# Attention weights of two heads in four turned by VectorE blocks and a DMA round trip

## The chip, the cores and the metric

One kernel runs on one core of one Trainium2 chip. The metric is the device time of a run in microseconds (us). A core has TensorE (PE in the profile; PEld is its loading of stationary operands), VectorE (DVE), ScalarE (ACT), GpSimd (POOL) and SyncE (SP), which issues nearly all of this kernel's DMAs. Everything is computed in 32-bit floats.

## The reference

The input x is 8 sequences of 256 tokens of 512 features; a second input is one row of 512 conditioning values per sequence. Four layers follow each other, each with a residual:

```
layer 0: h = rms-normed x, scaled by the condition
         q: 8 heads of 64, k and v: 1 head of 64 shared by all; rotary positions on q and k
         x += softmax(q k' / 8) v Wo
         x += (silu(h Wg) * (h Wu)) Wd                  inner width 2048
layer 1: h = layernorm(x), scaled and shifted by the condition
         q, k, v: 16 heads of 32;  q = q / |q| * exp(min(log scale, log 100)),  k = k / |k|
         x += gamma1 * (softmax(q k' + bias) v Wproj + b)
         x += gamma2 * (gelu(h Wfc1 + b) Wfc2 + b)      inner width 2048
layer 2: 16 query heads of 32, 4 key/value heads through a latent of 128, rotary, block mask
         x += softmax(masked q k') v Wo
layer 3: 8 experts of 64 features with an inner width of 256, layernorm, scale and shift, out projection
```

The bias of layer 1 is a 256x256 input. |q| and |k| are taken per head and token.

## The kernel before

All 8 sequences go through one stage after another: attention0, mlp0, attention1, mlp1, attention2, layer3. Activations x stay on the chip as 16 tiles of 128 tokens x 512 features. Tiles come from named pools, each with a number of slots (BUFS, L41): for instance "p" has 7 slots of 128x512, "ctxT" 6 of 128x256, "qk" 4, "wbig" 8 of 128x2048 for weights, and PSUM is split into "A" (4 banks, scores) and "C" (4 banks, all else). A tile that finds no free slot waits until the last reader of the oldest has finished. A scheduler orders the instructions of every engine from the order in which the program lists them and from the dependencies; within an engine they then run strictly in that order.

**The attention loop** (`attend`, L609) runs over sequences b and groups g of four heads: 2 groups a sequence in attention0, 4 in attention1 and attention2. For a group,

- `scored` (L645) multiplies queries by keys into four PSUM banks of 128 queries x (2 x 256 keys), one bank a head;
- `softmax` (L651) takes, per head and tile of 128 queries, the row's lowest value of minus the scores: one reduction on VectorE for attention0 (L659), a fused add-bias-and-minimum that also writes the negated scores to a "p" tile for the others (L667). ScalarE takes the exponential into "p" and sums the row (L672). The sums of the group are inverted (L678), turned (L682), and written to memory by a DMA (`spread`, L685), from which another DMA reads each row broadcast over a head's partitions (L690), into a free piece of a weight tile ("wqkv" in attention0, "wbig" later);
- `turned` (L697) turns one head's 128x512 weights on TensorE: four 128x128 transposes into a "C" bank (L702) and one copy back into the same "p" tile. The copy is on VectorE for even heads (L460) and on ScalarE for odd ones (L464);
- `weighted` (L709) multiplies the turned weights by the values (L717), and `divided` (L727) multiplies by the broadcast inverse into a "ctxT" tile (L732).

The loop is pipelined by hand. For each group it lists: scores of this group; the turning of the first two heads of the last group; the softmax of this group; a helping of other TensorE work; the turning of the last two heads of the last group; another helping; the weighted sum of the last group and its division; another helping. The helpings (`some`) draw on a queue of generators: the projections of the next sequence (`project0/1/2`), the output projection of the last one (`added` and the like), both with `product_steps` (L585). Each step of a generator tells its cost in us of TensorE; the helping is a fixed share of the sequence's total.

**The projection of attention1** (`project1`, L1334) handles two token tiles. For each it makes q, adds the bias, squares it on ScalarE (L1375) and sums per head on VectorE (L1376); then k, copied out of PSUM (L1373) and squared. The 16 sums of q and the 16 of k lie in one tile "ss" of 128x32. GpSimd takes the maximum with a small number, the power of minus one half (L1379) over all 32 columns, multiplies q's by its scale, and scales q and k (L1383). TensorE then turns q and k (L1355).

**The input of a stage** (`prepare`, L502) is normed x, features by tokens. For most sequences VectorE turns its 32x32 blocks in place (L515, 128x1024), four DMAs put it into memory (L520) and DMAs fetch it back so that the blocks stand where a full transpose would have them: one DMA of 512 KB for the MLPs (L533), eight of 64 KB for the attentions (L539). SP issues all of these in its own order, together with the spread DMAs and the loads of weights and x (L276).

**The MLPs** use a seven-product form of the 2x2 block product. Their right-hand operands are the pieces of hT and three sums of such pieces. The sums are kept in "ctxT" tiles, or in "qk" tiles for the first sequence (`blocked`, `blocked_again`). `mlp` (L892) makes the first products (L908), sums them in "p" tiles (`sums`, L922), and makes the second products (L955).

Of the kernel before, what the change touches and what calls it, by code (L numbers as in the profile page):

```python
# [32 lines left out]
P = 128  # L34
# [7 lines left out]
    "n": 4, "hT": 2, "qT": 2, "kT": 2, "v": 2, "ctxT": 6, "p": 7, "qk": 4, "row": 3, "wbig": 8,  # L42
# [46 lines left out]
PI_BELOW = 3.1415925  # L89

# [21 lines left out]
def layout(inputs):  # L112
# [10 lines left out]
    def grouped(w):  # L123
# [20 lines left out]
        "bias": np.ascontiguousarray(a["mask_1x1xSxS_ff0"].reshape(S, S)),  # L144
        "vec": np.ascontiguousarray(np.concatenate([vec[k] for k in VEC], 1)),
# [26 lines left out]
class Program:  # L172
# [50 lines left out]
    def setup(self):  # L223
# [40 lines left out]
        self.n_turn = 0  # L264
        self.half_pi = c([P, 1], "half_pi")
# [190 lines left out]
    def copy(self, i, out, in_, scale=None):  # L456

        if i % 2 == 0:
            if scale is None:
                self.nc.vector.tensor_copy(out, in_)  # L460
            else:
                self.nc.vector.tensor_scalar(out, in_, scale, None, ALU.mult)
        elif scale is None:
            self.nc.scalar.copy(out, in_)  # L464
        else:
            self.nc.scalar.activation(out, in_, AF.Copy, scale=scale)

    def modulated(self, i, out, in_, scale, shift):
        if shift is None:
            self.copy(i, out, in_, scale)  # L470
        elif i % 2 == 0:
            self.nc.vector.tensor_scalar(out, in_, scale, shift, ALU.mult, ALU.add)
        else:
            self.nc.scalar.activation(out, in_, AF.Identity, bias=shift, scale=scale)
# [27 lines left out]
    def prepare(self, name, b, quick=False):  # L502
# [14 lines left out]
        self.n_turn += 1  # L517
        to = kept.rearrange("(c i) (a x) -> a i c x", c=4, a=4)
        for a in range(4):
            nc.sync.dma_start(  # L520
                to[a], hT[32 * a : 32 * a + 32, :].rearrange("p (c x) -> p c x", c=4)
            )
        self.ready[name, b] = [hT, None, kept, 0]
# [17 lines left out]
    def h(self, name, b, quick=False):  # L541
# [16 lines left out]
        def placed(i, c, in_):  # L558
            scale = mod[:, scale_at + c, b : b + 1]
            shift = None if shift_at is None else mod[:, shift_at + c, b : b + 1]  # L560
            self.modulated(i, place[:, c], in_, scale, shift)

        if rows is None:
            for c in range(KC):
                placed(c, c, place[:, c])
# [43 lines left out]
    def attend(self, name, n_groups, hd, project, value, finish, work, key_tiles=(2, 2), biased=None,  # L609
# [27 lines left out]
        def scored(b, g):  # L637
# [3 lines left out]
            for j0 in range(0, 4, rows):  # L641
                for q in range(TB):
                    for j in range(j0, j0 + rows):
                        lhsT, rhs = lhs_rhs[j]
                        nc.tensor.matmul(  # L645
                            s[j][:, at[q] : at[q] + wide[q]], lhsT(q), rhs(wide[q]),
# [4 lines left out]
        def softmax(s):  # L651
            tot = self.t([P, 4, TB], "tot", 3)
            lows = self.t([P, 4, TB], "low", 3)
            ps = []
            for j in range(4):
                p = self.bank("p")[:, :total]
# [5 lines left out]
                for q in range(TB):  # L662
                    cols = slice(at[q], at[q] + wide[q])
                    src, sign = s[j], 1.0
                    if biased is not None:

                        nc.vector.tensor_tensor_reduce(  # L667
                            p[:, cols], s[j][:, cols], biased[:, cols], -1.0, BIG, ALU.add,
                            ALU.min, low[:, q : q + 1],
                        )  # L670
                        src, sign = p, -1.0
                    nc.scalar.activation(  # L672
                        p[:, cols], src[:, cols], AF.Exp, bias=low[:, q : q + 1], scale=sign,
                        accum_out=tot[:, j, q : q + 1],
                    )
                ps.append(p)
# [18 lines left out]
            return ps, by  # L695

        def turned(j, p):  # L697
# [9 lines left out]
            self.copy(j, p, m[:, :total])  # L707

        def weighted(b, g, pT):  # L709
            o = self.bank("C")  # L710
            for c in range(nch):
                for k in range(TB):
                    mine = [n for n, (kk, q) in enumerate(pairs) if kk == k]
                    q0 = pairs[mine[0]][1]
                    for i in range(per):
                        j = c * per + i
                        nc.tensor.matmul(  # L717
                            o[i * hd : (i + 1) * hd, c * S + q0 * P : (c + 1) * S],
                            value(got[b][1], g, j, k),
                            pT[j][:, mine[0] * P : (mine[-1] + 1) * P],  # L720
# [3 lines left out]
                        )  # L724
            return o
# [14 lines left out]
        for i in range(B * n_groups + 1):  # L740
# [17 lines left out]
            if last is not None:  # L758
                for j in range(2):
                    turned(j, last[2][0][j])  # L760
            if ahead is not None:
                ahead = (b, g, softmax(ahead[2]))
# [10 lines left out]
            elif ahead is None and then is not None:  # L773

                b, g, (pT, by) = last
                for j in range(2, 4):
                    turned(j, pT[j])
# [10 lines left out]
            else:  # L788
                self.some(quantum)
                b, g, (pT, by) = last  # L790
                for j in range(2, 4):
                    turned(j, pT[j])
# [58 lines left out]
    def blocked(self, b, hT):  # L851

        if b > 0:
            ts = [self.t([P, S], "ctxT") for _ in range(3)]
        else:

            ts = [t[:, i * S : (i + 1) * S] for t in (self.bank("qk"), self.bank("qk")) for i in range(2)]
            ts = ts[:3]
# [6 lines left out]
        return blocks  # L865

# [8 lines left out]
    def blocked_again(self, b):  # L875
# [3 lines left out]
        ts = [self.t([P, S], "ctxT") for _ in range(3)]  # L879
# [12 lines left out]
    def mlp(self, ups, downs, down_sums, load_ups, load_down, act, h, finish, tail):  # L892
# [29 lines left out]
        def sums(m):  # L922

            g = self.t([P, 4, P], "p")
# [4 lines left out]
            return g  # L929
# [69 lines left out]
        for s in range(n):  # L999
            hh, b, p = where(s)  # L1000
            w = ups[4 * hh + p]
            if p == 0:
# [4 lines left out]
                else:  # L1007
                    ms = [begun(i, x) for i in w]
                    gs = [sums(m) for m in ms]
# [10 lines left out]
            if s > 0:  # L1020
                ms = [begun(i, x) for i in w]
                gs = [sums(m) for m in ms]
# [213 lines left out]
    def layer0_mlp(self):  # L1236
# [52 lines left out]
        def finish(hh, b, ys):  # L1289
# [7 lines left out]
            (self.project1(0, self.got), 22.1),  # L1297
# [36 lines left out]
    def project1(self, b, got):  # L1334
# [28 lines left out]
        for t in range(TB):  # L1363
            ss = self.t([P, 32], "ss", 2)
            q = yield from part(t, 0)
            qs = self.bank("qk")
            nc.vector.tensor_tensor(qs, q, self.q_bias, ALU.add)
            sq = self.bank("n")
            nc.scalar.activation(sq, qs, AF.Square)
            nc.vector.tensor_reduce(ss[:, 0:16], heads(sq), AX.X, ALU.add)  # L1370
            k_ = yield from part(t, 1)
            ks = self.bank("qk")
            nc.scalar.copy(ks, k_)  # L1373
            sq = self.bank("n")
# [377 lines left out]
```

## Time and profile before

| what | value |
|---|---|
| median of 3 runs | 2128.06 us (2125.02 to 2128.92) |
| the profiled execution | 2125.73 us, its span 2123.8 us |
| granted TensorE clock, mean | 0.994 |
| moved by DMA | 138.18 MB |

| stage, us from the span's start | TensorE busy, us |
|---|---|
| start, 0 to 45 | 30.2 of 45 |
| attention0, 45 to 300 | 238.0 of 255 |
| mlp0, 300 to 890 | 590.0 of 590 |
| turn to layer 1, 890 to 920 | 28.8 of 30 |
| attention1, 920 to 1297 | 365.7 of 377 |
| mlp1, 1297 to 1667 | 370.0 of 370 |
| attention2, 1667 to 1975 | 293.2 of 308 |
| layer3, 1975 to 2124 | 144.6 of 149 |

A line of a group of instructions reads: line of the kernel, engine, operation, output<-input, partitions x elements, xcount | busy time in us, mean ns of one | idle time of the engine just before them, and what ended most of it. Matmuls overlap in TensorE's pipe, so the mean of one is longer than busy time over count. In a table of stretches each row has the stretch, its length, the busy time (and count) of PE, PEld, DVE, ACT and POOL, then TensorE's granted clock, the mean busy share of the 16 DMA engines and GB/s. A line of the timeline has the start, the duration of the piece, engine, line and what it is. A line of the waits has who waited for what, then us in total, times, the longest.

### The profile page before, as it was taken

The numbers are of one execution on the slowest core, as the hardware profiler recorded it, in microseconds if no ns is written. First come the engines' busy times: TensorE is split into PE (matmuls) and PEld (weight loads), VectorE is DVE, ScalarE is ACT, GpSimd is POOL, SyncE is SP. The second block draws the span as 40 slices with busy tenths as digits, with TensorE's granted clock in tenths as the row PEclk, the third lists the DMA queues.
The fourth block names the chain that finished last, engine by engine and source line by source line (L and its number), as shares of the span: only waits on it lengthen the run. The fifth ranks groups of instructions, "written<-read, shape, count | busy, mean of one in ns | idle before, by whom it ended". The sixth has DMA issues, their size and how long they took to land.

```text
span 2123.8 us, 36492 instructions
## 1 busy us (share of the span) xinstructions
PE 2060.5 (97%) x13282; PEld 1523.8 (72%) x13282; DVE 1349.5 (64%) x4474; ACT 761.1 (36%) x2330; POOL 291.3 (14%) x308
## 2 busy tenths in 40 slices
PE   7999899999999999999999999999999989999999
PEld 4555569999999999855555547999999855555444
DVE  6856665656676555756666665776666777776333
ACT  3424321111111111245555663222222256566644
POOL 1101100000000000144444432000000101010220
PEclk9999999999999999999999999999999999999999
DMA  8320241211230100411112132233211222210001
GB/s 308 115 59 17 91 149 38 73 41 58 76 94 19 36 19 18 100 46 40 37 40 52 44 95 78 85 102 115 94 49 46 76 47 45 57 39 19 11 35 40
DMA packets 172147, 138.18 MB, mean 65 GB/s; under 512 B 77824, under 2 KB 144064, under 8 KB 171968
## 3 DMA queue, kind: packets, MB, share of 16 engines
q1 hardware_dynamic: 171968, 135.86, 21.6%
q8 instruction: 105, 1.72, 0.3%
q14 instruction: 74, 0.61, 0.1%
HBM read 99.87 MB, written 35.95 MB: 64 GB/s over the span
## 4 chain that ended last, share of the span: by engine, by line
PE 81%; DVE 8%; DMA 5%; ACT 2%; POOL 2%; issue 1%; SPq 1%; DVEq 0%; ACTq 0%; POOLq 0%
PE C L908 28%; PE C L585 20%; PE A L955 18%; PE C L702 4%; PE A L645 4%; PE C L717 3%; DMA wqkv<-spread 2%; DVE p L667 1%; PE A L1621 1%; DMA spread<-invT 1%; ACT p L672 1%; PE C L1639 1%; DMA turn<-hT 1%; DMA hT<-turn 1%; DVE p L460 1%
## 5 line engine op out<-in xcount | busy, mean ns | idle before, releaser
L908 PE MATMUL C<-hT,wbig 128*128 128x128 f32 x3072 | 416.3, 275 | 0.0
L908 PEld LDWEIGHTS C<-hT,wbig 128*128 128x128 f32 x3072 | 388.8, 192 | 8.6 <-issue 1.8
L585 PE MATMUL C<-wqkv,hT 128*128 128x512 f32 (+1 forms) x768 | 311.1, 545 | 4.9 <-DVE p L460 3.9
L908 PE MATMUL C<-ctxT,wbig 128*128 128x128 f32 x2160 | 300.0, 275 | 0.0
L672 ACT ACTIVATE p<-p,low 128x256 f32<-128x256 f32 (+1 forms) x512 | 241.9, 475 | 152.7 <-DVE low L667 152.0
L908 PEld LDWEIGHTS C<-ctxT,wbig 128*128 128x128 f32 x2160 | 270.1, 192 | 0.0
L955 PE MATMUL A<-wbig,p 128*128 128x256 f32 x1024 | 242.5, 379 | 0.0
L585 PEld LDWEIGHTS C<-wqkv,hT 128*128 128x128 f32 x768 | 130.9, 191 | 124.7 <-issue 111.2
L667 DVE CUSTOM_DVE_ANT_0 p<-A,row 128x256 f32<-128x256 f32 (+1 forms) x512 | 171.7, 386 | 70.6 <-PE C L717 55.1
L955 PEld LDWEIGHTS A<-wbig,p 128*128 128x128 f32 x1024 | 189.6, 190 | 23.0
L702 PEld LDWEIGHTS C<-ident,p 128*128 128x128 f32 x1152 | 129.3, 142 | 81.3 <-issue 39.6
L925 ACT COPY p<-C 128x128 f32<-128x128 f32 x192 | 51.3, 267 | 371.6 <-PE C L908 370.9
L936 DVE TENSOR_TENSOR p<-p,C 128x256 f32<-128x256 f32 x192 | 79.3, 421 | 162.7 <-PE C L908 160.8
L702 PE MATMUL C<-ident,p 128*128 128x128 f32 x1152 | 165.2, 282 | 15.2 <-DVE p L460 6.8
L585 PE MATMUL C<-wo,ctxT 128*128 128x512 f32 x336 | 158.7, 604 | 5.6 <-DVE ctxT L732 5.5
L439 POOL TENSOR_SCALAR r<-mv 128x2 f32<-128x2 f32 (+1 forms) x28 | 7.2, 256 | 953.0 <-DVE mv L432 953.0
L1276 ACT ACTIVATE p<-C 128x128 f32<-128x128 f32 x64 | 17.8, 278 | 295.9 <-DVE p L936 295.9
L926 DVE TENSOR_TENSOR p<-p,C 128x128 f32<-128x128 f32 x192 | 54.9, 286 | 101.5 <-ACT p L925 99.4
L460 DVE COPY p<-C 128x512 f32<-128x512 f32 (+1 forms) x160 | 100.7, 630 | 23.8 <-PE C L702 23.4
L585 PEld LDWEIGHTS C<-wo,ctxT 128*128 128x128 f32 x336 | 58.7, 190 | 70.5 <-issue 53.8
L672 ACT ACTIVATE p<-A,low 128x256 f32<-128x256 f32 x128 | 59.3, 478 | 120.5 <-DVE low L659 87.9
L464 ACT COPY p<-C 128x512 f32<-128x512 f32 (+1 forms) x160 | 85.5, 535 | 36.0 <-PE C L702 36.0
(226 smaller groups left out, 3064.7 us busy)
## 6 DMA issues: line engine op xcount, KB each, us to landing
turn<-hT SPq DMA_DIRECT2D x120, 128.0 KB
hT<-turn SPq DMA_DIRECT2D x16, 512.0 KB
kept<-hT SPq DMA_DIRECT2D x16, 512.0 KB
hT<-kept SPq DMA_DIRECT2D x16, 512.0 KB
wbig<-spread SPq DMA_DIRECT2D x64, 128.0 KB
hT<-turn SPq DMA_DIRECT2D x112, 64.0 KB
wbig<-in_wada1T SPq DMA_DIRECT2D x6, 1024.0 KB
ctxT<-kept SPq DMA_DIRECT2D x48, 128.0 KB
```

Source lines behind the costliest of these rows:

```text
L460: self.nc.vector.tensor_copy(out, in_)
L464: self.nc.scalar.copy(out, in_)
L585: self.nc.tensor.matmul(out, lhsT(k), rhs(k), start=(k == 0), stop=(k == n - 1))
L645: nc.tensor.matmul(s[j][:, at[q] : at[q] + wide[q]], lhsT(q), rhs(wide[q]), start=True, stop=True,)
L667: nc.vector.tensor_tensor_reduce(p[:, cols], s[j][:, cols], biased[:, cols], -1.0, BIG, ALU.add, ALU.min, low[:, q : q + 1],)
L672: nc.scalar.activation(p[:, cols], src[:, cols], AF.Exp, bias=low[:, q : q + 1], scale=sign, accum_out=tot[:, j, q : q + 1],)
L702: nc.tensor.transpose(m[:, n * P : (n + 1) * P], p[:, at[q] + k * P : at[q] + (k + 1) * P], self.ident,)
L717: nc.tensor.matmul(o[i * hd : (i + 1) * hd, c * S + q0 * P : (c + 1) * S], value(got[b][1], g, j, k), pT[j][:, mine[0] * P : (mine[-1] + 1 ...
L908: nc.tensor.matmul(m[:, c : c + P], w[:, k * P : (k + 1) * P], b[:, k], start=(first and k == 0), stop=(k == steps - 1), skip_group_check= ...
L926: nc.vector.tensor_tensor(g[:, 0, :], g[:, 0, :], m[:, P : 2 * P], ALU.add)
L936: nc.vector.tensor_tensor(g[:, 1:3, :], g[:, 0, :].unsqueeze(1).to_broadcast([P, 2, P]), m[:, 2 * P : 4 * P].rearrange("p (i t) -> p i t", ...
L955: nc.tensor.matmul(acc[at][:, half * S : (half + 1) * S], left, right, start=(p == 0 and half == 0), stop=(p == 3), skip_group_check=True,)
```

## The change

In attention0 and attention1, for all sequences but the last, the first two heads of each group (`in_blocks`) are no longer turned by TensorE.

- `scored` multiplies these heads by keys in a permuted order (a strided view of the key tile).
- `softmax` writes their exponentials interleaved into one "p" tile of 128x1024, in four chunks of 64 columns for each query tile. VectorE turns its 32x32 blocks in place, four DMAs of 128 KB put it into memory (`put`, shared now with `prepare`), and one DMA of 512 KB reads it back into the same tile. These instructions are listed right after the softmax steps of the third head and before those of the fourth.
- `weighted` reads these heads' weights through a strided view of that tile (runs of 32), and these matmuls are kept in program order.
- `turned` is called once where it was called twice, and its remaining copies both go to ScalarE in those groups. Where no head is in blocks, the copies alternate as before.
- attention1's bias is needed in the permuted order too: a second copy (`bias_blocks`, prepared with the other inputs) is loaded into a piece of a weight tile of layer 1 that is free during the attention.

Around it: "p" has 4 slots of 128x1024 instead of 7 of 128x512; a group takes two, one for the heads in blocks and one for the others. The MLPs and layer3 take a pair of 128x512 tiles as one slot. "ctxT" goes from 6 slots to 4, and the MLPs' three operand sums take "ctxT" for odd sequences and "qk" for even ones (`three`). `layer1_begin` runs the first projection of attention1 and then loads one of layer 1's down weights and the bias; the other weights of layer 1 follow in the order ups, downs. In `h`, the in-place scalings of the input are kept in program order.

In `project1` the norms are apart: for q, and then for k, squares, sums, maximum, power over 16 columns and scaling follow each other at once. k's squares are taken from PSUM.

```diff
-    "n": 4, "hT": 2, "qT": 2, "kT": 2, "v": 2, "ctxT": 6, "p": 7, "qk": 4, "row": 3, "wbig": 8,
+    "n": 4, "hT": 2, "qT": 2, "kT": 2, "v": 2, "ctxT": 4, "p": 4, "qk": 4, "row": 3, "wbig": 8,
...
+    def in_blocks(self, name, b):
+        return 2 if name != "attention2" and b < B - 1 else 0
+
+    def put(self, kept, tile):
+        to = kept.rearrange("(c i) (a x) -> a i c x", c=4, a=4)
         for a in range(4):
-            nc.sync.dma_start(
-                to[a], hT[32 * a : 32 * a + 32, :].rearrange("p (c x) -> p c x", c=4)
+            self.nc.sync.dma_start(
+                to[a], tile[32 * a : 32 * a + 32, :].rearrange("p (c x) -> p c x", c=4)
             )
...
+                        keys = rhs(wide[q])
+                        if j < self.in_blocks(name, b):
+                            keys = keys.rearrange("p (k c i) -> p c k i", c=4, i=32)
                         nc.tensor.matmul(
-                            s[j][:, at[q] : at[q] + wide[q]], lhsT(q), rhs(wide[q]),
+                            s[j][:, at[q] : at[q] + wide[q]], lhsT(q), keys,
...
+            blocks = self.t([P, 8 * P], "p")[:, : 2 * total]
+            if n_blocks:
+                put = blocks.rearrange("p (c h x) -> p h c x", c=4, h=2)
+                ps = []
+            else:
+                ps = [blocks[:, j * total : (j + 1) * total] for j in range(2)]
+            plain = self.t([P, 2, 512], "p")
+            ps += [plain[:, j, :total] for j in range(2)]
...
-                ps.append(p)
+                if j == n_blocks == 2:
+                    nc.vector.transpose(blocks, blocks)
+                    kept = self.flips[self.n_flip % 4][:, : 2 * total]
+                    self.n_flip += 1
+                    self.put(kept, blocks)
+                    nc.sync.dma_start(blocks, kept)
...
+            came = blocks.rearrange("p (a h n j) -> p h n a j", a=4, h=2, j=32)
+            def weights(j, mine):
+                if j < self.in_blocks(name, b):
+                    ns = [at[pairs[n][1]] // P + pairs[n][0] for n in mine]
+                    step = ns[1] - ns[0] if len(ns) > 1 else 1
+                    return came[:, j, ns[0] : ns[-1] + 1 : step]
+                return plain[j - self.in_blocks(name, b)][:, mine[0] * P : (mine[-1] + 1) * P]
...
             if last is not None:
-                for j in range(2):
-                    turned(j, last[2][0][j])
+                weights = last[2][0][1]
+                for j, p in enumerate(weights[: len(weights) // 2]):
+                    turned(j + len(weights) % 4 // 2, p)
...
+    def three(self, b):
+        if b % 2 == 1:
+            return [self.t([P, S], "ctxT") for _ in range(3)]
+        two = [self.bank("qk") for _ in range(2)]
+        return [two[0][:, :S], two[0][:, S:], two[1][:, :S]]
...
+            both = []
+            for i in range(2):
+                m = yield from part(t, i)
+                y = self.bank("qk")
+                sq = self.bank("n")
+                if i == 0:
+                    nc.vector.tensor_tensor(y, m, self.q_bias, ALU.add)
+                    nc.scalar.activation(sq, y, AF.Square)
+                else:
+                    nc.scalar.activation(sq, m, AF.Square)
+                    nc.scalar.copy(y, m)
+                r = ss[:, 16 * i : 16 * i + 16]
+                nc.vector.tensor_reduce(r, heads(sq), AX.X, ALU.add)
+                nc.gpsimd.tensor_scalar(r, r, 1e-24, None, ALU.max)
+                nc.gpsimd.tensor_tensor(r, r, self.neg_half[:, 0:16], ALU.pow)
+                if i == 0:
+                    nc.gpsimd.tensor_tensor(r, r, self.sm, ALU.mult)
+                by = r.unsqueeze(2).to_broadcast([P, 16, 32])
                 nc.gpsimd.tensor_tensor(heads(y), heads(y), by, ALU.mult)
+                both.append(y)
...
+    def layer1_begin(self):
+        yield from self.project1(0, self.got)
+        self.ups, self.downs = [], []
+        self.layer1_down(0)
+        self.bias_blocks = self.downs[0][3]
+        self.nc.sync.dma_start(
+            self.bias_blocks.rearrange("p (q k) -> p q k", q=TB),
+            self.d["bias_blocks"].rearrange("(q p) k -> p q k", p=P),
+        )
```

## What the change does to the time: a prediction

> **What bounds the kernel now.** I read four views in this order: the page's shares and its chain that ended last, the busy table by stretches of time, the costliest groups, and the timeline of one group of heads.
>
> ```profile
> span 2123.8 us, 36492 instructions
> PE 2060.5 (97%) x13282; PEld 1523.8 (72%) x13282; DVE 1349.5 (64%) x4474; ACT 761.1 (36%) x2330; POOL 291.3 (14%) x308
> ...
> PE C L908 28%; PE C L585 20%; PE A L955 18%; PE C L702 4%; PE A L645 4%; PE C L717 3%; DMA wqkv<-spread 2%; DVE p L667 1%; PE A L1621 1%; DMA spread<-invT 1%; ACT p L672 1%; PE C L1639 1%; DMA turn<-hT 1%; DMA hT<-turn 1%; DVE p L460 1%
> ```
>
> TensorE works 97% of the span and its lines lead the chain; L702, the transposes of softmax weights, is itself 4% of it. Work taken off TensorE therefore shortens the end unless a wait takes its place.
>
> The shares are means over stages. In the two attentions that change (45 to 300 us and 920 to 1297 us) the table gives, per stretch, busy PE, PEld, DVE, ACT, POOL:
>
> ```profile
> 45.00:300.00 255.00, 238.04 (x1379) 142.17 (x1378) 171.10 (x483) 90.38 (x299) 36.88 (x63) 0.99 0.26 78
> ...
> 920.00:1297.00 377.00, 365.73 (x2138) 195.29 (x2135) 239.75 (x834) 213.13 (x663) 156.76 (x116) 0.99 0.20 52
> ```
>
> Here too PE leads: idle 17 us of 255 in the first and 11 of 377 in the second; DVE is at 67% and 64%, ACT at 35% and 57%, the DMA engines at 0.26 and 0.20. The second has 32 groups, so 11.8 us a group, of which DVE needs 7.5 and ACT 6.7. There is room for PE to get 1 us shorter per group before either becomes the bound.
>
> ```profile
> L702 PE MATMUL C<-ident,p 128*128 128x128 f32 x1152 | 165.2, 282 | 15.2 <-DVE p L460 6.8
> L515 DVE STREAM_TRANSPOSE hT<-hT 128x1024 f32<-128x1024 f32 x30 | 37.1, 1236 | 0.3
> L460 DVE COPY p<-C 128x512 f32<-128x512 f32 (+1 forms) x160 | 100.7, 630 | 23.8 <-PE C L702 23.4
> L464 ACT COPY p<-C 128x512 f32<-128x512 f32 (+1 forms) x160 | 85.5, 535 | 36.0 <-PE C L702 36.0
> ```
>
> **Part 1, the transposes removed.** Four heads a group need 16 transposes; two heads in blocks need 8 fewer. Attention0 has 2 groups and attention1 has 4 for each of seven sequences: 14 + 28 = 42 groups, 336 transposes. What one costs is read from the timeline (start, duration):
>
> ```profile
> 1100.45 1.15 PE L645 MATMUL A<-kT,qT 32*128 32x256 f32 x16
> 1101.52 1.09 PE L702 MATMUL C<-ident,p 128*128 128x128 f32 x8
> 1102.45 1.04 PE L1355 MATMUL C<-ident,qk 128*128 128x128 f32 x8
> ...
> 1120.45 1.07 PE L717 MATMUL C<-p,v 128*32 128x256 f32 x16
> ```
>
> Eight take from 1101.52 to the next start at 1102.45, 0.93 us or 116 ns each. The group's busy time over its count, 165.2/1152, is 143 ns. The 282 ns is the latency of one in the pipe. The Trainium skill ("TensorE: Matmul & The Clock Gate", Part 4: PE-mode transpose) gives about 275 ns for one in a kernel; that matches the latency column and would make the saving 336 x 0.275 = 92 us. The step between starts decides what a queue of them costs, so I take 0.117: **-39 us**, with 48 (at 143 ns) as the other end.
>
> The same skill speaks against the change: "VectorE: DVE Perf Modes", Rules for kernel authors, says to turn 128x128 on TensorE where PSUM will do, since VectorE turns only 32x32 blocks. In total work the row agrees: 8 transposes are 0.93 us of PE and two evacuations, while the new way is 1.24 us of DVE plus 1 MB of DMA. By the rule the change loses; by the shares above it trades the full engine's time for idle ones', so I follow the shares.
>
> **Part 2, VectorE and ScalarE.** Per group one DVE block transpose of 128x1024 is added (L515's own shape, 1.24 us). Of the four evacuations two go, and the remaining pair both goes to ACT: DVE loses two at 0.63 us = 1.26, ACT keeps its two. Net 0 for both. The chunked operands of L667, L672, the keys of L645 and the moving weights of L717 read runs of 32 elements. That such runs cost PE nothing shows in L908, which reads the input in runs (hT) and whole (ctxT):
>
> ```profile
> L908 PE MATMUL C<-hT,wbig 128*128 128x128 f32 x3072 | 416.3, 275 | 0.0
> ...
> L908 PE MATMUL C<-ctxT,wbig 128*128 128x128 f32 x2160 | 300.0, 275 | 0.0
> ```
>
> 416.3/3072 = 136 ns against 300.0/2160 = 139: nothing. For DVE and ACT no row compares the two; I take nothing, at most 10% of a group's four L667 and four L672 (4 x 0.35 + 4 x 0.50 = 3.4 us), 0.3 us, hidden under PE's 10.9.
>
> **Part 3, the trip through memory.** After the block transpose, SP issues four puts of 128 KB, then a read of 512 KB into the same tile; the weighted sum (L717) waits for it. The MLP inputs already make this trip in the same shapes; SP's rows there and the chain's row for such a read:
>
> ```profile
> 333.82 1.77 SPq L520 DMA_DIRECT2D turn<-hT  x4
> 337.55 0.34 SPq L533 DMA_DIRECT2D hT<-turn  x1
> ```
>
> ```profile
> 244.39 7.70 DMA turn<-hT
> 252.18 3.94 DMA hT<-turn
> ```
>
> From the first put to the read's issue 3.73 us, then 3.94 to landing. With 1.24 of DVE that is 8.9 us. In the timeline the exps of the first two heads end 3.6 us after the scores begin (1104.06), and DVE may first be at the third head's L667: some 4 to 4.5. A block is back 13 to 13.5 us after its group's scores begin. Before, the weighted sum starts 1120.45 - 1100.45 = 20.0 us after the scores. I summed the PE work that the changed order puts between the two, at the row durations: attention0 14.4, 36.5, then 15 to 28 us; attention1 14.6 for the first group, then 16.4 to 26.9, and 12.9 to 21.8 in the last sequence in blocks. So mostly the trip is hidden under PE's other work (L585 above all). If that cover is gone each group costs what is missing, up to the whole 8.9. Tight places:
> - attention0's first group (14.4): SP is still issuing loads of x until 40.1 us, ahead of the puts. I take +3 (0 to 6).
> - attention1's first group (14.6): +1 (0 to 3).
> - attention1's last block sequence (12.9 and 15.9): +3 together (0 to 5).
> The 7.70 row is a put that came slowly while other transfers ran. Such a trip, 13 us, would be late for most groups; one in seven is a guess worth 0 to 6, counted in the range alone.
>
> **Part 4, SP's queue.** Five more issues a group, about 0.45 each, 210 in all. A put waits for DVE, and the read for its puts; behind it stand the spread reads (L690) of the divisors and the fetches of the next input (L533/L539). In the middle of the second attention a set of eight fetches stands between the first put and the others, in the group with 26.9 us of cover: nothing. A spread read held back about 2 us hurts only where it is on the path already: the chain has wqkv<-spread at 2% of the span, reads of 7.9 to 8.1 us in attention0, and L732 waited 14.7 us for them in 5 places. Before PE runs dry the cover is ctxT's; I take +3 (0 to 8). The bytes: 42 MB more; 1 MB a group at the 338 GB/s of the first 45 us is 3.1 us per 10.9, raising the DMA share from 0.20 to under 0.5.
>
> **Part 5, buffers.** p becomes four pairs instead of seven singles, and a group's fourth head no longer takes the slot that the previous weighted sum frees:
>
> ```profile
> DVE p L667 <- PE C L717: 55.1, 44, 2.8
> ```
>
> That is DVE's wait. The chain gives DVE p L667 about 1.5% of the span (32 us), but this is its work as well as its wait, with PE still 97% busy; I take -2 (0 to -8). ctxT from six to four, with the MLP's operands alternating between ctxT and qk, and the pairs in the last layer: L908 has no idle before it; 0 (to +3).
>
> **Part 6, norms apart.** POOL's power on 128x32 takes 5.45 us (L1379), on the critical chain twice at attention1's start (897.90 and 906.00). Two of 128x16 halve the last: by L1379 at 32 columns and L440's 0.71 to 0.74 us at 2, 0.16 us a column, so 2.9 us. By then q's are done, and the scaled k is ready some 2.5 to 4 us sooner, with 2 x 1.05 of scaling (L1383) also split; elsewhere it is hidden: **-3** (0 to -4). The order of the layer1 loads and the 256 KB of permuted bias lie under the first MLP: 0.
>
> **Sum.** -39 -3 -2 +7 +3 = -34. The profiled execution took 2125.73 us (span 2123.8); 2125.7 - 34 = 2091.7. The median of the runs shown, 2128.06, is 2.3 above it: **2094**. Its own range: with 48 for the transposes, -5, and half of the delays, 2125.7 - 48 + 2.3 = 2080; with 39, -5, and every delay at its upper end (6 + 3 + 5 + 8 = 22), 2106.
>
> **Rivals.**
> - *The trip outlasts its cover (slower).* PE waits at the weighted sum in most groups because the puts and the read take as long as that 7.70 row plus 3.94, 13 us with the transpose, so blocks come back 18 us after the scores against a cover of 16 to 18. The gain of 44 over 42 groups is used up at a mean wait of 1.05 us; at 2 us it is 84 - 44 = +40, 2168. For: 512 KB out and in again per group, on the one queue that feeds everything. Against: the MLP trips of the same shape took 7.7 us in all.
> - *Gain lost to other engines.* PE becomes shorter, but in-order waits for ACT's copies (now both on one engine) and exps take most of it, since L702 already waited 15.2 us. At half a microsecond in each of 42 groups, 21: 2115. For: ACT's exps lag DVE by 0.5 us a head.
> - *More gain.* 143 ns a transpose and the freed p slot worth 8: -48 -8 -3 +5 = -54, 2074.
> That the change doesn't do what it says is excluded: the changed order lists eight fewer transposes in each of the 42 groups.
>
> **Numbers.** 0.2% (4 us) is about what a measurement of this kernel tells from no change. Likeliest 0.55; more gain 0.13; gain lost 0.13 (2106 to 2123); about equal 0.03; slower 0.16. Faster 0.81, same 0.03, slower 0.16. 2072 to 2130 leaves out the slower case and a part of the higher gain.
>
> **What would show it.** L702's count 816, its busy time near 117; the two stretches shorter by some 10 and 25 us; PE's idle time before L717 (3.0 + 1.0 us now) below 12 in all with the block's read as releaser. The prediction is wrong if that wait is over 40 us, if a spread read or fetch on SP's queue stops L732 or L585 in every sequence, or if L667 or L672 have become longer by over a tenth.

## The result: 2155.04 us, 1.3% slower

| kernel | median of the runs | profiled span | granted clock, mean |
|---|---|---|---|
| before | 2128.49 us (2125.02 to 2130.22) | 2123.8 us | 0.994 |
| changed | 2155.04 us (2152.83 to 2161.6) | 2154.1 us | 0.980 |

The ratio is 1.0132 (95% interval 1.0106 to 1.0158): 28 us slower, where 2094 us and a gain of 34 were forecast. The head of the changed kernel's page and its chain by line:

```profile
span 2154.1 us, 36247 instructions
PE 2074.1 (96%) x12946; PEld 1506.0 (70%) x12946; DVE 1347.1 (63%) x4432; ACT 750.3 (35%) x2330; POOL 303.4 (14%) x340
...
PE C L963 28%; PE C L599 21%; PE A L1012 18%; ACT p L705 6%; PE C L765 3%; PE A L663 3%; PE C L740 2%; PE A L1692 1%; POOL ss L1439 1%; DVE p L701 1%; PE C L1711 1%; DVE st L440 1%; ACT p L472 1%; PE C L315 1%; DVE n L618 0%
```

TensorE has 336 instructions less and is busy 14 us more. The exponentials on ScalarE (L705), 1% of the chain before (L672), are 6%. The groups that the prediction sized came out as it sized them:

```profile
L740 PE MATMUL C<-ident,p 128*128 128x128 f32 x816 | 122.2, 281 | 4.9 <-DVE p L469 2.0 <-ACT qT L473 1.5 <-ACT p L705 0.8
L710 DVE STREAM_TRANSPOSE p<-p 128x1024 f32<-128x1024 f32 x42 | 52.2, 1243 | 6.3 <-ACT p L705 5.8
L1439 POOL TENSOR_TENSOR ss<-ss,neg_half 128x16 f32<-128x16 f32 x32 | 93.6, 2926 | 2.7
```

816 transposes with 43 us less of busy time, a block transpose of 1.24 us, a power of 2.93. So the loss is elsewhere. By stretches (the columns are those of the first tables: PE, PEld, DVE, ACT, POOL, then clock and DMA):

```profile
0.00:284.30 284.30, 251.51 (x1370) 145.49 (x1370) 197.85 (x566) 105.23 (x344) 43.76 (x84) 0.96 0.53 168
910.50:1291.30 380.80, 364.38 (x1878) 176.74 (x1877) 239.81 (x806) 209.22 (x662) 164.32 (x142) 0.96 0.46 124
1704.50:2002.40 297.90, 275.65 (x1818) 155.27 (x1817) 196.65 (x883) 161.48 (x616) 32.45 (x40) 0.95 0.16 37
```

The stretches run from the start to the first MLP's first product, from attention1's first scores to the second MLP, and over attention2 to its last weighted sum. Before, the same three took 291.4, 368.6 and 273.3 us. The first gained 7. Attention1, with two thirds of the removed transposes, lost 12; attention2, where no head is in blocks, lost 24.6. And the clock fell: a mean of 0.980 over 2154 us is some 86 us at one half, against 26 before.

Where one sequence of attention1 begins, TensorE's and then ScalarE's timeline show the hole:

```profile
1158.34 1.15 PE L663 MATMUL A<-kT,qT 32*128 32x256 f32 x16
1159.42 1.98 PE L599 MATMUL C<-wqkv,hT 128*128 128x512 f32 x4
1161.33 1.78 PE L663 MATMUL A<-kT,qT 32*128 32x256 f32 x8
1164.40 1.22 PE L663 MATMUL A<-kT,qT 32*128 32x256 f32 x4 [1.29 <-DVE low L701]
1165.55 7.95 PE L599 MATMUL C<-wqkv,hT 128*128 128x512 f32 x12
```

```profile
1160.67 0.51 ACT L705 ACTIVATE p<-p,low 128x256 f32<-128x256 f32 x1 [1.54 <-DVE low L701]
...
1164.38 0.51 ACT L705 ACTIVATE p<-p,low 128x256 f32<-128x256 f32 x1 [0.16 <-DVE low L701]
1164.89 1.08 ACT L480 ACTIVATE hT<-hT,mod 128x256 f32<-128x256 f32 x2
```

The projection of the next sequence (L599 at 1165.55) needs that sequence's scaled input, half of which ScalarE makes (L480). ScalarE does so only after the eight exponentials of the group. Until then, but for the four products on VectorE's half (L599 at 1159.42), TensorE has no other work than the scores of the second group, drawn up behind those of the first; these wait for VectorE to empty the four score banks. The clock in and after that stretch:

```profile
1160.40:1163.80 3.40, 2.71 (x11) 1.06 (x9) 3.32 (x15) 3.13 (x13) 0.00 (x0) 1.00 0.36 127
1163.80:1167.20 3.40, 2.80 (x6) 1.34 (x7) 0.96 (x5) 2.00 (x6) 0.00 (x0) 0.51 0.61 153
1167.20:1170.60 3.40, 3.40 (x5) 1.35 (x4) 0.00 (x0) 0.00 (x0) 0.00 (x0) 0.50 0.64 196
```

It is half for the next two of these pieces, though TensorE is full in the second of them. In the kernel before, ScalarE scaled the same input at 1123.66 and 1126.35, a good 30 us before the scores at 1159.11.

One line of the diff ties the scaling there: `keep_in_program_order` on `placed`, in `h`, called the edge from here on. The scaling is listed after the softmax of the first group, and with the edge it can't move ahead.

### The profile page after: what moved, and what is told of

Same layout as the page of the kernel before. It is cut to its first block, busy times and chain, and to the rows that moved or that the text cites. A ratio compares the mean times of both kernels' runs of the same rounds, so it can differ in the third digit from the quotient of the medians.

```text
span 2154.1 us, 36247 instructions
## 1 busy us (share of the span) xinstructions
PE 2074.1 (96%) x12946; PEld 1506.0 (70%) x12946; DVE 1347.1 (63%) x4432; ACT 750.3 (35%) x2330; POOL 303.4 (14%) x340
## 4 chain that ended last, share of the span: by engine, by line
PE 79%; ACT 7%; DVE 7%; POOL 3%; DMA 2%; issue 1%; SPq 0%; ACTq 0%; DVEq 0%; POOLq 0%
PE C L963 28%; PE C L599 21%; PE A L1012 18%; ACT p L705 6%; PE C L765 3%; PE A L663 3%; PE C L740 2%; PE A L1692 1%; POOL ss L1439 1%; DVE p L701 1%; PE C L1711 1%; DVE st L440 1%; ACT p L472 1%; PE C L315 1%; DVE n L618 0%
## 5 line engine op out<-in xcount | busy, mean ns | idle before, releaser
L599 PE MATMUL C<-wqkv,hT 128*128 128x512 f32 (+1 forms) x768 | 327.6, 568 | 2.6 <-ACT hT L480 1.4
L705 ACT ACTIVATE p<-p,low 128x256 f32<-128x256 f32 (+1 forms) x512 | 240.4, 471 | 160.4 <-DVE low L701 153.4
L599 PEld LDWEIGHTS C<-wqkv,hT 128*128 128x128 f32 x768 | 136.2, 200 | 133.3 <-issue 116.8
L599 PE MATMUL C<-wo,ctxT 128*128 128x512 f32 x336 | 157.7, 603 | 2.7 <-DVE ctxT L782 2.7
L963 PE MATMUL C<-qk,wbig 128*128 128x128 f32 x1152 | 160.0, 275 | 0.0
L963 PE MATMUL C<-ctxT,wbig 128*128 128x128 f32 x1152 | 160.0, 275 | 0.0
L701 DVE CUSTOM_DVE_ANT_0 p<-A,row 128x256 f32<-128x256 f32 (+1 forms) x400 | 128.9, 376 | 43.6 <-PE C L765 29.4
L963 PEld LDWEIGHTS C<-qk,wbig 128*128 128x128 f32 x1152 | 144.1, 192 | 0.0
L963 PEld LDWEIGHTS C<-ctxT,wbig 128*128 128x128 f32 x1152 | 144.1, 192 | 0.0
L740 PEld LDWEIGHTS C<-ident,p 128*128 128x128 f32 x816 | 93.0, 142 | 64.9 <-issue 40.8
L740 PE MATMUL C<-ident,p 128*128 128x128 f32 x816 | 122.2, 281 | 4.9 <-DVE p L469 2.0
L663 PE MATMUL A<-kT,qT 32*128 32x256 f32 (+2 forms) x896 | 105.6, 404 | 16.2 <-DVE low L701 12.5
L663 PEld LDWEIGHTS A<-kT,qT 32*128 32x128 f32 (+1 forms) x896 | 62.4, 191 | 67.0 <-issue 37.2
```

Source lines behind the costliest of these rows:

```text
L599: self.nc.tensor.matmul(out, lhsT(k), rhs(k), start=(k == 0), stop=(k == n - 1))
L663: nc.tensor.matmul(s[j][:, at[q] : at[q] + wide[q]], lhsT(q), keys, start=True, stop=True,)
L701: nc.vector.tensor_tensor_reduce(out, src, by, -1.0, BIG, ALU.add, ALU.min, low[:, q : q + 1])
L705: nc.scalar.activation(out, src, AF.Exp, bias=low[:, q : q + 1], scale=sign, accum_out=tot[:, j, q : q + 1],)
L740: nc.tensor.transpose(m[:, n * P : (n + 1) * P], p[:, at[q] + k * P : at[q] + (k + 1) * P], self.ident,)
L963: nc.tensor.matmul(m[:, c : c + P], w[:, k * P : (k + 1) * P], b[:, k], start=(first and k == 0), stop=(k == steps - 1), skip_group_check= ...
```

## The experiments

Theory A: the edge costs the time. Theory B: the blocks cost it (their trip through memory, their tiles). Every kernel here computes the whole reference. Ratios are to the kernel before on the same chip; 0.1% is 2.1 us.

### The edge added to the old kernel, and taken from the new one

old_pin, the kernel before with these lines and the change's `three`:

```diff
-    ... "ctxT": 6, "p": 7, ...
+    ... "ctxT": 4, "p": 8, ...
-                placed(c, c, place[:, c])
+                self.tc.keep_in_program_order(placed(c, c, place[:, c]))
```

> The kernel before with one new thing: the in-place scaling of a stage's input is kept in program order (to be schedulable at all it gets one more p slot, 8 instead of 7, and ctxT 4 with the changed kernel's sharing of operand sums). No head is in blocks and the norms are together. Theory A (the program-order edge on the scaling makes the scheduler pull the second group's scores of each sequence up behind the first's; TensorE then waits for VectorE to empty the score banks, and its clock drops): attention2 longer by about 21 us as in the changed kernel, attention1 longer by 15 to 25, half-clock time some 45 us more; 2160 to 2172 us. Theory B (the loss comes with the blocks: their DMA trip, their pair tiles): 2124 to 2132.

2183.06 us, 1.0259 (1.0238 to 1.028). Theory A, and more than it asked for: attention1 took 396.9 us, attention2 296.5. But half-clock time rose by 28 us only (mean clock 0.987 over 2177.4), where 45 were expected. What the slots have of the loss comes below.

new_unpinned, the changed kernel with:

```diff
-                self.tc.keep_in_program_order(placed(c, c, place[:, c]))
+                placed(c, c, place[:, c])
```

> The changed kernel with that one program-order edge taken away, all else as changed. Theory A: attention2 back to about 268 us and attention1 down from 381 to about 345 to 355; 2105 to 2120 us. Theory B: 2150 to 2160, attention1 still near 381 us.

2112.8 us, 0.9939 (0.9915 to 0.9963). One line is worth 1.9%, 41 us; without it the change is a gain. Attention1 falls from 380.8 to 348.5 us, attention2 from 297.9 to 281.5:

```profile
913.90:1262.40 348.50, 342.30 (x1880) 169.05 (x1879) 243.50 (x806) 207.55 (x662) 164.03 (x142) 0.99 0.51 138
1675.60:1957.10 281.50, 260.42 (x1818) 144.53 (x1817) 196.19 (x883) 159.31 (x616) 32.36 (x40) 0.98 0.17 40
```

new_noblocks, the changed kernel with `in_blocks` returning 0:

> The changed kernel with no head in blocks anywhere: TensorE turns all four heads, no trip through memory; slots, program-order edges and norms as changed. Theory A: attention2 stays near 290 us, attention1 near 390; 2155 to 2172 us. Theory B: about the time before, 2120 to 2132.

2186.77 us, 1.0276 (1.0252 to 1.0299). Slower than with blocks, by 31 us: theory B falls. It was above theory A's range too.

### Is it the scores drawn up, or the late scaling?

new_ordered, the changed kernel with:

```diff
-                        nc.tensor.matmul(
+                        self.tc.keep_in_program_order(nc.tensor.matmul(
                             s[j][:, at[q] : at[q] + wide[q]], lhsT(q), keys,
                             start=True, stop=True,
-                        )
+                        ))
...
-        nc.scalar.activation(sin[0], ang, AF.Sin, scale=-1.0)
+        self.tc.keep_in_program_order(nc.scalar.activation(sin[0], ang, AF.Sin, scale=-1.0))
```

(the latter for all four activations of `angles`)

> The changed kernel with the matmuls of the scores kept in program order too, and the four sine and absolute-value activations of the angle tables kept in program order on ScalarE (in the changed kernel they stand ahead of the copy of v and ScalarE waits 16.4 us there, TensorE 10.3). Blocks stay. Theory A: no pulled scores, half-clock time back to about 30 us, no 10 us hole near 60 us; the 39 us of transposes then show: 2090 to 2105 us. Theory B: only the hole at the start goes; 2138 to 2148 us.

2176.34 us, 1.0228 (1.021 to 1.0246): a miss, slower than the changed kernel. With the scores held back, TensorE simply stands until the scaling is done. Its wait for it before the projections, changed kernel first, then new_ordered:

```profile
PE C L599 <- ACT hT L480: 3.4, 6, 1.6
```

```profile
PE C L599 <- ACT hT L480: 29.0, 7, 4.3
```

Nor did half-clock time fall: it is 92 us (mean clock 0.979 over 2173.6). So scores drawn up are what the scheduler fills the hole with, and a little help; the late scaling makes the hole. The theory had the right line of the diff and the wrong link.

scaled_early keeps the edge and lists the scaling earlier:

```diff
             if ahead is not None:
+                if g == 0 and ahead_of and 0 < b < B - 1:
+                    next(self.queue[0])
                 ahead = (b, g, softmax(ahead[2], b))
```

> The changed kernel, its program-order edge on the input's scaling kept, but in attention1 and attention2 the scaling is listed before the softmax of a sequence's first group instead of after it. Theory A2 (the edge costs because the scaling must stand behind that group's eight exps on ScalarE, so the next sequence's projection comes late and TensorE has nothing else): the loss goes though the edge stays, 2105 to 2120 us, no half-clock stretch per sequence. Theory A1 (any such edge ties the engines' order too tightly): 2145 to 2160 us.

2106.74 us, 0.99 (0.9883 to 0.9916): 48 us less than the changed kernel, with the edge in place. Its timeline at the same point of the work:

```profile
1136.17 1.09 ACT L480 ACTIVATE hT<-hT,mod 128x256 f32<-128x256 f32 x2
1136.36 0.27 PE L740 MATMUL C<-ident,p 128*128 128x128 f32 x1
1136.57 1.15 PE L663 MATMUL A<-kT,qT 32*128 32x256 f32 x16
1137.64 2.84 PE L599 MATMUL C<-wqkv,hT 128*128 128x512 f32 x6
...
1138.20 0.51 ACT L705 ACTIVATE p<-p,low 128x256 f32<-128x256 f32 x1 [0.93 <-DVE low L701]
```

Scaling, scores, projection, and the exponentials meanwhile. The half-clock time is 44 us in place of 86.

### What the blocks, the norms and the slots are worth

unpinned_noblocks is new_unpinned with `in_blocks` returning 0.

> The changed kernel without the edge and with no head in blocks: what is left are the slots, the load order and the norms apart. If the prediction's term for the transposes is right (336 at 0.117 us less a few us of waits, 30 to 40 us between this and the same with blocks at 2112.8): 2140 to 2153 us. If the trip and the waits eat half of it: 2125 to 2135 us. If these other parts cost nothing it is at the time before, 2128.

2155.74 us, 1.0129 (1.0112 to 1.0147), against 0.9939 with blocks: 1.9%, 40 us, where the prediction's term for the transposes was 39. But with neither blocks nor edge the rest of the change costs 27 us, though its norms gain. So the 40 are what the blocks are worth beside that rest, not the transposes alone.

unpinned_norms_together is new_unpinned with `project1` as before.

> The changed kernel without the edge, and with the norms of queries and keys together as before. If the norms apart are worth the 3 us of the prediction at attention1's start: 2114 to 2118 us. If POOL's latency was hidden: 2110 to 2114 us.

2120.82 us, 0.9962 (0.9947 to 0.9977) against 0.9939 (0.9915 to 0.9963): about 5 us for the norms apart, with intervals that overlap. The expectation counted from the 2112.8 of another chip's runs; the ratios are what compares.

old_slots is the kernel before with 8 p slots, ctxT 4 and `three`; old_ctxT4 the same with 7 p slots:

```diff
-    ... "ctxT": 6, "p": 7, ...
+    ... "ctxT": 4, "p": 8, ...      (old_slots)
+    ... "ctxT": 4, "p": 7, ...      (old_ctxT4)
```

> The kernel before with 8 single p slots instead of 7, ctxT 4 instead of 6 and the shared operand sums of the MLPs; nothing else. unpinned_noblocks took 27 us more than the kernel before though its norms are worth 8 us less. If the freer slots are what costs it (groups run ahead, and the copies and divisions meet in VectorE's queue): 2145 to 2165 us. If it is the pair tiles or the load order of layer 1: 2126 to 2131 us.

> The kernel before with ctxT 4 instead of 6 slots and the shared operand sums of the MLPs, p left at 7. If the eighth p slot cost the 25.7 us of old_slots (TensorE's order here is that of the kernel before): 2124 to 2131 us, within 0.2% of before. If ctxT did: 2145 to 2152 us.

old_slots: 2150.77 us, 1.0114 (1.0099 to 1.0129). old_ctxT4: 2130.15 us, 1.0004 (0.9995 to 1.0013). So one more p slot, 2 KB a partition more to work in, costs the kernel before some 23 us. The edge alone, old_pin against old_slots, costs it 31. Who waits for whom, kernel before first, then old_slots:

```profile
PEld C L717 <- ACT p L464: 4.3, 9, 0.8
DVE ctxT L732 <- PE C L717: 6.2, 6, 1.6
```

```profile
PEld C L717 <- ACT p L464: 28.0, 38, 1.3
DVE ctxT L732 <- PE C L717: 35.1, 34, 3.8
```

With the slot free, the fourth head's exponentials no longer wait for the last group's weighted sum; they run ahead of the last group's copies in ScalarE's order, and the weighted sum (L717) waits for those copies. The matmuls of the weighted sums show it, kernel before first, then old_slots, then new_unpinned:

```profile
L717 PE MATMUL C<-p,v 128*32 128x256 f32 (+2 forms) x896 | 69.3, 370 | 3.0 <-DVE p L460 3.0
L717 PE MATMUL C<-p,kT 128*32 128x128 f32 (+2 forms) x384 | 34.2, 351 | 1.0 <-DVE p L460 1.0
```

```profile
L717 PE MATMUL C<-p,v 128*32 128x256 f32 (+2 forms) x896 | 81.6, 375 | 8.0 <-DVE x L1197 3.5 <-ACT p L464 2.9 <-DVE p L460 0.3
L717 PE MATMUL C<-p,kT 128*64 128x256 f32 (+2 forms) x384 | 36.9, 359 | 3.2 <-ACT p L464 2.4 <-DVE p L460 0.5
```

```profile
L765 PE MATMUL C<-p,v 128*32 128x256 f32 (+2 forms) x896 | 81.1, 372 | 7.7 <-ACT p L472 4.6 <-DMA p<-flip 1.7 <-DVE p L469 0.3
L765 PE MATMUL C<-p,kT 128*64 128x256 f32 (+2 forms) x384 | 36.7, 356 | 4.0 <-ACT p L472 3.9
```

Busy and idle time together are 107.5, 129.7 and 129.5 us. The same matmuls cost 22 us more in both; in unpinned_noblocks, where the slots are free too, they come to 127.2.

slots_back is early_first_plain (next part) with p's slots as tight as before:

```diff
-    ... "ctxT": 4, "p": 4, ...
+    ... "ctxT": 6, "p": 3, "pb": 2, ...
-            blocks = self.t([P, 8 * P], "p")[:, : 2 * total]
+            blocks = self.t([P, 8 * P], "pb")[:, : 2 * total]
-            plain = self.t([P, 2, 512], "p")
...
+                if j >= 2:
+                    ps.append(self.bank("p")[:, :total])
```

(the MLPs and layer3 take pairs and singles in turn)

> early_first_plain (0.9889 of before) with p's slots as tight as before: two pairs for the heads in blocks and three singles for the others, so that a group's fourth head again waits for the weighted sum before it; ctxT 6. If freer slots cost the changed kernel too (exps of the next group stand ahead of the copies and the division of the last): 5 to 20 us less than early_first_plain, the weighted sums back to 63 and 49 ns a matmul; 2082 to 2096 us. If only the kernel before, with more copies, pays for them: 2098 to 2104 us.

2108.88 us, 0.9909 (0.9894 to 0.9925) against 0.9889 (0.9868 to 0.9911): no gain. Attention1 and attention2 took 2.6 and 4.6 us less in the profile, but the stretch to the first MLP took 7 us more and that from the first MLP to attention1's scores another 7. The weighted sums did become cheap again: 105.2 us busy, against 118.7 in early_first_plain. But TensorE now waits for what comes from memory, for the block's reads and for divisions that wait for their spread reads:

```profile
PE C L599 <- DVE ctxT L782: 11.9, 6, 4.3
...
PE C L765 <- DMA pb<-flip: 7.1, 5, 3.0
```

In early_first_plain these were 2.0 and 0.3 us. So with blocks in, tight slots save at one place and lose as much at others: the slots that let the groups run ahead seem to be also what covers the trip. That rests on this one arrangement of the slots, with ctxT back at 6 besides.

slots_back_copy moves the second copy of a group with blocks to VectorE; slots_back_unpinned drops the edge and lists the scaling late again.

> slots_back with the second copy of a group with blocks on VectorE. If the copies' wait on ScalarE came from the freer slots: within 3 us of slots_back. If it is ScalarE's own load: 3 to 6 us less than slots_back.

> slots_back without the edge on the scaling and with the scaling listed where the changed kernel has it. If the edge costs only through its place: within 4 us of slots_back. If ScalarE and VectorE wait in order for a scaling whose DMA is late (26.9 us in 16 places in new_unpinned): 4 to 10 us more than slots_back.

2103.44 us, 0.9888 (0.987 to 0.9905); and 2117.6 us, 0.9953 (0.9938 to 0.9968). The copy's 0.2% lies within the intervals. The edge, with the scaling listed early, is worth 9 us against no edge: here a fixed place ahead of the exponentials is better than the place that the scheduler chose. And slots_back_unpinned, which has neither edge nor freed slots, is only 10 us faster than the kernel before, of which the norms have some 5. By that estimate, from three ratios, the blocks are worth about 5 us with tight slots, against the 40 with free ones.

### The first sequence and the copies

In the changed kernel TensorE stands 10.3 us near 57 us. unpinned_sine is new_unpinned with the activations of `angles` kept in program order.

> The changed kernel without the edge on the scaling, and with the four activations of the angle tables kept in program order on ScalarE. If ScalarE's 16 us wait for them is what makes TensorE stand 10.3 us near 57 us: that hole and half of its 10 us at half clock go, 2098 to 2104 us. If TensorE would wait there for the weights' trip anyway: 2109 to 2114 us.

2113.84 us, 0.9931 (0.9916 to 0.9946): no change. The copy of v came at once, and TensorE stood 8.43 us one step later, for VectorE's division (L782). In the changed kernel that division, of the first group, reads:

```profile
54.51 1.95 PE L765 MATMUL C<-p,kT 128*64 128x256 f32 x16
...
65.21 0.36 DVE L1153 TENSOR_SCALAR row<-row 128x384 f32<-128x384 f32 x1
65.48 0.75 DVE L782 TENSOR_TENSOR ctxT<-C,wqkv 128x256 f32<-128x256 f32 x2
```

Its weighted sum starts at 54.51 and its spread reads were issued at 47.77; the reads that SP issues late, at 58.69, are the second group's. VectorE works without a break from 53.73 up to the division: it stands behind the angle tables (L1133 to L1153) in VectorE's order. Why the scheduler puts it there is not shown. early_first_plain is scaled_early with the first sequence of attention0 turned by TensorE; early_first_copy adds the second copy on VectorE:

```diff
-        return 2 if name != "attention2" and b < B - 1 else 0
+        return 2 if name != "attention2" and b < B - 1 and (name, b) != ("attention0", 0) else 0
...
                 for j, p in enumerate(weights[len(weights) // 2 :]):
-                    turned(j + len(weights) % 4 // 2, p)
+                    turned(j, p)                         (early_first_copy)
```

> The kernel with the scaling listed early (2106.7 us against 2129.4 before), and with the very first sequence of attention0 turned by TensorE alone, as the last one is. If the first groups' trip, behind the loads of x on SP's queue, is what holds back the spread reads (issued at 59 us) and with them VectorE's division and TensorE for 10.3 us, plus the half clock after it: the hole near 57 us and 5 to 10 us of half clock go, 2092 to 2099 us. If the hole is due to the angle tables on VectorE and ScalarE alone: 2105 to 2110 us.

> As early_first_plain, and in groups with blocks the second of the two copies of turned weights goes to VectorE, the first stays on ScalarE. The weighted sums of attention1 take 77 ns a matmul in the middle and 108 in the upper quarter where 63 is undisturbed, some 9 us in the stage. If they wait for ScalarE's second copy, behind its exps: 5 to 9 us less than early_first_plain. If they wait for the block's read from memory: the same within 2 us, and the 108 ns stay.

2101.47 us, 0.9889 (0.9868 to 0.9911), and 2097.02 us, 0.9865 (0.9847 to 0.9882), on one chip with 2125.03 before. The hole is gone, and the first group's division comes at 59.19, but the stretch to the first MLP is only 3.4 us shorter in the profile (281.0 against 284.4); by the ratios the run can't be told from scaled_early. The copy's 4.4 us lie within the intervals too; but the weighted matmuls of attention1 are busy 40.5 us where they took 44.8 (37.6 before), so part of their wait was ScalarE's copy and not the read. early_first_copy beats both kernels, by 1.35% the one before.

## Why the prediction was wrong

**The step that failed first is not in the sum.** The edge on the input's scaling was told of with the change and priced nowhere: part 2 asked what VectorE and ScalarE have to do, not what stands ahead of what on them. It costs 41 us with blocks (1.0132 against 0.9939) and 31 without (1.0276 against 1.0129), enough to turn -34 into a loss.

**It is not the whole miss.** Without the edge the change gains 13 us of the 34. The 21 that are missing are of the size of the 22 us more at the weighted sums, which part 5 had with the wrong sign; that the two are the same is read from the traces, not tested. A rival, "gain lost to other engines", foresaw this part: it said 2115 us by in-order waits for ScalarE's copies and exponentials, and new_unpinned took 2112.8. None of the rivals was the edge.

**Part 1 was right on the transposes themselves.** L740's busy time is 43 us less, against 39. That 40 us lie between unpinned_noblocks and new_unpinned is in part luck, since the worth of the blocks depends on the slots. In both pairs that differ in the blocks alone, with the edge (31 us) and without, the blocks gain: the rule to turn on TensorE does not hold here, where TensorE is full.

**Part 2.** The rates were right. L701 in chunks, whose bias lies in wbig, takes 419 ns, and 418 whole; L705 takes 497 on average (501 before), and in attention0, where almost half of it is in chunks, 485 (478 before). So chunks of 64 in runs of 32 cost next to nothing. "Net 0" for the copies was not right: both copies on ScalarE wait behind its exponentials. early_first_copy puts that at some 4 us, within the noise.

**Part 3 was right for the changed kernel, and the slower rival wrong.** TensorE waited for a block's read once:

```profile
PE C L765 <- DMA p<-flip: 0.5, 1, 0.5
```

That is not because the trip is always short. The last one, beside weight loads of attention2, has its first put at 1249.18 and lands 10.0 us later, where 7.7 was estimated:

```profile
1250.54 4.15 DMA flip<-p
1254.77 4.37 DMA p<-flip
```

The cover held. With tight slots (slots_back) it did not quite: TensorE waits 7.1 us for the reads there. The +3 of the first sequence compares with 3.4 in early_first_plain, but what stood there was a division in VectorE's order, so that agreement is luck.

**Part 4.** The +3 was not seen. VectorE waited 10.3 us for spread reads in the changed kernel, and 23.0 before.

**Part 5 had the sign wrong.** A freed slot was entered as -2 us because a wait of VectorE would go. That wait kept the order of the groups: without it the weighted sums cost 22 us more, in the kernel before (old_slots) as in the changed one without the edge. What giving the slot back would net with blocks in is not settled, since slots_back then pays at the reads.

**Part 6.** -3; about -5 measured, not apart from -3 by the intervals.

The shares of the 41 us: between the profiles of the changed kernel and new_unpinned TensorE has the same matmuls, its busy time falls by 36 us and its idle time by 10 (the spans differ by 45). Half-clock time falls by some 35 us (mean clock 0.980 over 2154.1 and 0.988 over 2108.8), which is at most 18 us of work. The other 23 or so are waits for the scaling and for the score banks, part of them inside what counts as busy, as where eight score matmuls take 1.78 us at 1161.33 and sixteen take 1.15 at 1158.34. This split is worked out from the clock, not tested on its own.

Left open: some 8 us of unpinned_noblocks beyond the slots (24) and the norms (-5), which may be the pair tiles or the order of layer 1's loads; the other edge of the change, on the weighted matmuls of the heads in blocks, which no run takes away; and why attention2, which has no blocks, still takes 278.4 us in scaled_early against 273.3 before. There 277.7 in old_slots and 273.9 in slots_back point to the slots.

## What to carry to other kernels

Where a scheduler orders the engines, price every edge and every freed slot of a change by what it moves on the in-order queues: list what stands ahead of each input that the fullest engine reads, before and after. An edge that keeps program order is only as good as the place in the program; put work that feeds the next stage ahead of the longest run on its engine. A wait that a buffer causes may be what keeps the groups in order, so removing it is not a gain by itself. And what one part of a change is worth can hang on another, as the blocks do on the slots: a sum of parts measured one at a time need not come out.

## What was not expected of the hardware

TensorE was never idle for more than 1.3 us at a time in the stretch shown from 1157 to 1166 us, and the clock was halved after it, for 6.8 us. The Trainium skill ("TensorE: Matmul & The Clock Gate", Why this matters for your kernels) warns of gaps of more than about 3 us. Here two groups of score matmuls on 32 of 128 rows came ahead of the drop, with 2.7 us busy in the piece of 3.4 shown; two such groups stand ahead of each of the six drops of attention1 in the changed kernel. The same two groups with the same gap of 1.29 us, at 1113.75 and 1116.82, were followed by none, so they are not enough by themselves. Which of the two, the few rows or the short gap, tips it was not tried.
